# Query products of a two-layer graph transformer as pairs of tiles in seven quadrant products

## The chip, the core and the metric

The kernel runs on one core of a Trainium2 chip. The metric is device time in microseconds (us). The core has five engines that run their own streams of instructions and meet through semaphores: TensorE (PE; its weight loads are shown apart, as PEld), VectorE (DVE), ScalarE (ACT), GpSimd (POOL) and SyncE (SP), which here only issues DMA transfers. Operands lie in SBUF, 128 partitions wide; matmuls write into eight PSUM banks of 128 x 512 float32.

## The reference, cut to what matters

Two layers, each graph attention and a feed-forward block, on N = 2708 tokens of width 512, with 8 heads of 64 and a hidden width of 2048, all in float32. The adjacency matrix is sparse and differs per token.

```python
def layer(h, adj, Wq, bq, Wk, bk, Wv, bv, Wo, bo, W1, b1, W2, b2, ...):
    mask = adj.astype(float32) + eye(n)
    q = (h @ Wq.T + bq).reshape(n, 8, 64)
    k = (h @ Wk.T + bk).reshape(n, 8, 64)
    v = (h @ Wv.T + bv).reshape(n, 8, 64)
    scores = einsum('nhd,mhd->hnm', q, k) / sqrt(64)
    scores = where(mask[None] == 0, -1e9, scores)
    ctx = einsum('hnm,mhd->nhd', softmax(scores), v).reshape(n, 512)
    h1 = layer_norm(h + ctx @ Wo.T + bo, ln1_g, ln1_b)
    ff = relu(h1 @ W1.T + b1) @ W2.T + b2
    return layer_norm(h1 + ff, ln2_g, ln2_b)

x = layer(x, adj, *layer0);  x = layer(x, adj, *layer1)
```

The change touches only `q = h @ Wq.T + bq` with its factor of 1/8.

## The kernel before, in words

`by_edges` holds both layers. The tokens are 22 tiles of 128 (the last one has 20). For every token the kernel makes a list of its neighbours from the adjacency matrix, sorts the tokens by the length of their lists, and regroups them into 22 groups of like length. Attention then gathers the keys and values of a group's neighbours, two slots (`SLOTS`) at a time, from a table `kv_d` in DRAM; queries go through a table `q_d` in DRAM, and a group fetches the rows of its tokens. The order of all instructions is written out by hand: generators for attention (`attend`, moved on by `advance` and `until`), the feed-forward and the norms are interleaved with the products, and each engine runs its instructions in the order in which the Python code issues them. A tile pool with `bufs=n` has n buffers per tag; who asks for a buffer waits until everything that used it, transfers too, is through.

The work goes through these stages (times are those of the trace before):

- *Keys of layer 0* (0 to 154 us, `first`). A pair of tiles at a time, `xg` is loaded from the transposed input by SP (three buffers, tags w1_5 to w1_7; `load`, line 921). PE makes keys and values (`project`, line 616), ACT takes them out of PSUM, POOL adds the key bias (line 964), ACT's queue stores them to `kv_d`. Beside that `lists` (line 729) works on the adjacency rows: SP loads a half row block `aj` (line 737), POOL adds the diagonal (line 740), ACT turns it into codes (line 746), DVE finds the neighbours with MAX8 (line 751). At t = 19 to 21 `counted` and `ranked` (lines 766 and 827) sort the tokens: DVE's chain from line 772 to 813, and then a product on PE, `pr` (line 841), behind which PE's later work stands.
- *Queries of layer 0* (about 154 to 250 us, `first_queries`, line 996). `xg` is loaded a second time, each tile is one product of 4 x 128x512 by `wq`, DVE scales it by 1/8 and adds `bq` in one instruction (`evicted`, line 1001; `bq` is scaled once when it is loaded), two tiles share a buffer `qs` and are stored together. At t = 2 the last keys and the lists' placing are finished, and from then on attention of layer 0 is moved on between the tiles.
- *Feed-forward of layer 0* (250 to about 1050 us): 11 blocks of two groups, `blocks`, with the attention of the next block between its steps. Most of them already use a form with seven quadrant products (`feed_forward_by_seven`, line 1734). Each block's result gets its layer-1 keys and values one block later (`keys_values`, line 1858), which also stores its transposed tokens `zT` to `zT_d` in DRAM.
- *The border* (about 1050 to 1145 us): the last block's keys and values, then the queries of layer 1. Their tokens come back from `zT_d`; the first eight tiles are loaded ahead (`preloaded`, line 1428), others follow in streams of three (`queries`, line 1448). `query` (line 1462) is one tile: product, one eviction into a buffer `qs` with the tag `row` (three buffers, used by the residual rows of the feed-forward as well), and behind it `kept` (line 1475) issues the store of the tile before. Weights of the coming feed-forward are formed on DVE (`form_apart`, line 1688). Attention of layer 1 starts here (`next(ahead)`). Twenty of the 22 tiles are asked for here; the two of the block that ended last are asked for beside the first feed-forward block.
- *Feed-forward of layer 1* (1145 to 1815 us), like layer 0's.

An attention step (`Tile.weights` and `Tile.weigh`, lines 1154 and 1169) is a product of keys and queries on DVE (line 1156), a sum (1162), exponentials on ACT, products with values on ACT and DVE (1182, 1188) and an addition on DVE (1195).

These few lines carry the query path before:

```python
def evicted(t, q, qs):                                   # layer 0, line 1001
    nc.vector.scalar_tensor_tensor(
        qs[:r, t % 2], q[:r], DK**-0.5, bq[:r], ALU.mult, ALU.add)
...
qs = dn.tile([P, DM], F32, tag="row", name="qs", bufs=3) # layer 1, line 1462 on
nc.vector.scalar_tensor_tensor(qs[:r], q[:r], DK**-0.5, self.bq[:r], ALU.mult, ALU.add)
self.kept()
self.due = (g, qs)
```

Of the kernel before, what the change touches and what calls it, by code (L numbers as in the profile page):

```python
# [18 lines left out]
P = 128  # L19
# [27 lines left out]
OWN = 5  # L47
WARM = 7
# [439 lines left out]
def by_edges(ctx: ExitStack, tc: tile.TileContext, x, xT, adj, layers, out, redo):  # L488
# [150 lines left out]

    def finish(steps):  # L640
        for _ in steps:
            pass
# [274 lines left out]
    def first(w, meanwhile):  # L917
# [3 lines left out]
        def load(by=nc.sync):  # L921
# [5 lines left out]
            step = bw if i else P  # L927
            for a in range(0, bw, step):
                (by if a else nc.sync).dma_start(
                    out=t[:, :, a : a + step], in_=chunked(xT)[:, :, b + a : b + a + step]  # L930
                )
                yield
# [20 lines left out]
        done, before = 0, None  # L953
        for t in range(NT):
# [27 lines left out]
            meanwhile(t)  # L982
            if t == QT:
                wq = matrix(w, "Wq", "wq", nc.gpsimd)
            if t == NT - 4:
                bq = row_of(short[1], "bq", DK**-0.5)

# [6 lines left out]
        return bq, wq, parts, placing[1], pa, tokens, last_keys  # L994

    def first_queries(bq, wq, parts, inverted, pa, tokens, last_keys, meanwhile):

        nonlocal at
        made = []

        def evicted(t, q, qs):
            r = size(t)
            nc.vector.scalar_tensor_tensor(
                qs[:r, t % 2], q[:r], DK**-0.5, bq[:r], ALU.mult, ALU.add
            )
            plus_rest(qs[:r, t % 2], q, r, DK**-0.5)
# [11 lines left out]
        for t in range(NT):  # L1018
            r = size(t)
            q = project(tokens(t, 1), r, wq, "q", other=t % 2 > 0)  # L1020
# [18 lines left out]
            evicted(t, q, qs)  # L1039
# [33 lines left out]
    def own_query(g, zT, to, bq, wq):  # L1073
# [3 lines left out]
        nc.vector.scalar_tensor_tensor(to[:r], q[:r], DK**-0.5, bq[:r], ALU.mult, ALU.add)  # L1077
        plus_rest(to[:r], q, r, DK**-0.5)
# [279 lines left out]
    class Layer:  # L1358
        def __init__(self, n, w):
            self.n, self.w, self.w1, self.w2, self.due = n, w, [], [], None  # L1360
            self.stages = []
            self.apart, self.other = True, False
# [65 lines left out]
        def preloaded(self, tiles, temp):  # L1428

            places = []  # L1430
            for _ in range(2):
                both = at.tile([P, SLOTS, DM], F32, tag="acc", name="zTs", bufs=2)
                places += [both[:, i] for i in range(SLOTS)]
            places += [at.tile([P, DM], F32, tag="cx", name="zTs", bufs=CXB) for _ in range(CXB)]
            places.append(temp())
            places = [place.rearrange("p (c t) -> p c t", c=NC) for place in places]
            for g, place in zip(tiles, places):
                nc.sync.dma_start(out=place, in_=zT_d[self.n][g])
            return list(zip(tiles, places))

        def two(self, tiles):

            both = dn.tile([P, 2, NC, P], F32, tag="hT", name="zTs", bufs=1)
            for i, g in enumerate(tiles):
                nc.sync.dma_start(out=both[:, i], in_=zT_d[self.n][g])
            return both

        def queries(self, tiles):

            zTs = []  # L1450
            for i in range(len(tiles) + 1):
                while len(zTs) < min(i + 3, len(tiles)):
                    zT = dn.tile([P, NC, P], F32, tag="cT", name="zT", bufs=3)
                    nc.sync.dma_start(out=zT, in_=zT_d[self.n][tiles[len(zTs)]])
                    zTs.append(zT)
                yield
                if i < len(tiles):
                    self.query(tiles[i], zTs[i])
            self.kept()
            yield  # L1460

        def query(self, g, zT):
# [3 lines left out]
            q = project(lambda c: zT[:, c, :r], r, self.wq, "q", self.other and self.apart)  # L1466
            qs = dn.tile([P, DM], F32, tag="row", name="qs", bufs=3)
            nc.vector.scalar_tensor_tensor(
# [786 lines left out]
```

## Time and profile before

| | before |
|---|---|
| median of 3 runs | 1817.35 us (1817.26 to 1817.72) |
| the profiled execution | 1817.08 us, span of its instructions 1815.1 us |
| PE, matmuls | 1791.5 us busy, 99% of the span |
| PEld, weight loads | 1214.6 us, 67% |
| DVE | 1463.3 us, 81% |
| ACT | 1001.1 us, 55% |
| POOL | 855.4 us, 47% |
| DMA | 426.74 MB, mean 235 GB/s |
| mean granted clock of TensorE | 0.998 |

The span is the time from the first to the last instruction of the profiled execution; its own time is 2 us longer. Busy times are sums over the engine's instructions, those that only issue a transfer not counted. In the rows below, a timeline row has its start and its busy time in us, then the engine, the line of the kernel, the operation, its output and inputs by the program's names with their sizes, and the number of instructions put together; what stands in brackets at its end is the idle time ahead of it and what ended that. A row of a window has its length, then for PE, PEld, DVE, ACT and POOL the busy time and the count, the granted clock, the DMA share and GB/s. A row of transfers has the issuing queue and the number of issues, KB of each, and the median time from issue to landing.

### The profile page before, as it was taken

The numbers are of one execution on the slowest core, as the hardware profiler recorded it, in microseconds if no ns is written. First come the engines' busy times: TensorE is split into PE (matmuls) and PEld (weight loads), VectorE is DVE, ScalarE is ACT, GpSimd is POOL, SyncE is SP. The second block draws the span as 40 slices with busy tenths as digits, with TensorE's granted clock in tenths as the row PEclk, the third lists the DMA queues.
The fourth block names the chain that finished last, engine by engine and source line by source line (L and its number), as shares of the span: only waits on it lengthen the run. The fifth ranks groups of instructions, "written<-read, shape, count | busy, mean of one in ns | idle before, by whom it ended". The sixth has DMA issues, their size and how long they took to land. (4 is left out here: it accounts for less than half of the span.)

```text
span 1815.1 us, 23887 instructions
## 1 busy us (share of the span) xinstructions
PE 1791.5 (99%) x6839; PEld 1214.6 (67%) x6839; DVE 1463.3 (81%) x2599; ACT 1001.1 (55%) x3397; POOL 855.4 (47%) x830
## 2 busy tenths in 40 slices
PE   9999999999999999999999999999999999999997
PEld 4444456666777867777677644666666888788786
DVE  4987778988989889799896267988888899989933
ACT  5771436645555555555653104677776677767631
POOL 3333755534454544454540132556665665655312
PEclk9999999999999999999999999999999999999999
DMA  9997987757676675666752777967867787877531
GB/s 335 369 344 252 374 284 245 230 181 241 203 238 220 203 259 192 208 220 202 241 194 73 242 285 272 319 193 256 279 186 263 243 264 237 293 225 234 173 94 36
DMA packets 186728, 426.74 MB, mean 235 GB/s; under 512 B 20550, under 2 KB 83898, under 8 KB 186584
## 3 DMA queue, kind: packets, MB, share of 16 engines
q0 software_dynamic: 76992, 264.49, 44.0%
q1 hardware_dynamic: 99434, 139.01, 22.5%
q10 hardware_dynamic: 10158, 21.61, 3.1%
q8 instruction: 56, 0.92, 0.2%
q14 instruction: 88, 0.72, 0.1%
HBM read 357.13 MB, written 57.11 MB: 228 GB/s over the span
## 5 line engine op out<-in xcount | busy, mean ns | idle before, releaser
L1119 POOL DMA_INDIRECT kv<-kv_d,listed x420 | 526.0, 1252 | 307.2 <-DVE acc L1195 145.8
L1780 PE MATMUL pf<-hT,w 128*128 128x256 f32 x1792 | 407.2, 379 | 2.1 <-ACT ft L1791 2.1
L1780 PEld LDWEIGHTS pf<-hT,w 128*128 128x128 f32 x1792 | 339.2, 190 | 59.2 <-issue 11.0
L1182 ACT ACTIVATE kv<-kv,p 128x64 f32<-128x64 f32 x1232 | 311.0, 335 | 5.0
L1156 DVE TENSOR_TENSOR kv<-kv,q 128x1024 f32<-128x1024 f32 (+1 forms) x222 | 257.1, 1158 | 14.1 <-DMA q<-q_d,ident_i 10.9
L1162 DVE TENSOR_REDUCE sc<-kv 128x16 f32<-128x1024 f32 (+1 forms) x222 | 258.0, 1162 | 7.6
L1195 DVE TENSOR_TENSOR acc<-acc,kv 128x1024 f32<-128x1024 f32 (+2 forms) x178 | 205.6, 1155 | 49.6 <-ACT kv L1182 36.9
L1596 PEld LDWEIGHTS pf<-hT,w 128*128 128x128 f32 x1024 | 178.5, 190 | 55.3 <-issue 34.6
L1596 PE MATMUL pf<-hT,w 128*128 128x256 f32 (+1 forms) x1024 | 214.6, 357 | 0.1
L1791 ACT ACTIVATE ft<-pf,b 128x256 f32<-128x256 f32 x168 | 78.1, 466 | 214.1 <-PE pf L1780 211.4
L1569 PE MATMUL a<-w,ft 128*128 128x512 f32 x416 | 194.6, 592 | 0.0
L1175 ACT ACTIVATE p<-sc,listed 128x8 f32<-128x8 f32 x420 | 103.6, 295 | 127.9 <-DVE sc L1162 116.5
L1281 POOL TENSOR_TENSOR rd<-va,mhalf 128x1 f32<-128x1 f32 (+1 forms) x48 | 43.8, 913 | 230.8 <-DVE va L1279 230.7
L626 PE MATMUL o<-wo,cT 128*128 128x512 f32 x336 | 151.0, 593 | 0.3 <-ACT cT L1354 0.3
L1188 DVE TENSOR_TENSOR kv<-kv,p 128x512 f32<-128x512 f32 (+1 forms) x178 | 123.6, 694 | 4.8 <-ACT p L1175 4.5
L1569 PEld LDWEIGHTS a<-w,ft 128*128 128x128 f32 x416 | 77.7, 190 | 57.5 <-issue 52.0
L626 PEld LDWEIGHTS o<-wo,cT 128*128 128x128 f32 x336 | 63.4, 190 | 69.3 <-issue 59.6
L1331 POOL TENSOR_SCALAR va<-sq 128x1 f32<-128x1 f32 (+1 forms) x40 | 17.2, 429 | 188.4 <-ACT xb L1324 101.9
L751 DVE MAX8 tops<-code 128x8 f32<-128x247 f32 (+2 forms) x242 | 78.8, 400 | 28.0 <-ACT code L746 27.9
L1226 ACT ACTIVATE cx<-acc,su 128x64 f32<-128x64 f32 (+1 forms) x352 | 88.2, 333 | 11.2 <-DVE su L1218 6.2
L1182 ACT ACTIVATE acc<-kv,p 128x64 f32<-128x64 f32 (+1 forms) x352 | 88.8, 335 | 1.4
L746 ACT ACTIVATE code<-aj 128x1354 bf16<-128x1354 int32 (+1 forms) x44 | 73.5, 1724 | 23.7 <-POOL aj L740 19.0
(258 smaller groups left out, 2793.8 us busy)
## 6 DMA issues: line engine op xcount, KB each, us to landing
forms<-form_d SPq DMA_DIRECT2D x294, 128.0 KB, 3.8
aj<-in_adj SPq DMA_DIRECT2D x42, 677.0 KB, 6.3
kv_d<-kvs ACTq DMA_DIRECT2D x21, 512.0 KB, 7.4
h<-ln_b POOLq DMA_DIRECT2D x41, 256.0 KB, 7.0
xg<-in_xT SPq DMA_DIRECT2D x19, 512.0 KB, 8.0
w<-in_W SPq DMA_DIRECT2D x16, 512.0 KB, 6.4
kv<-kv_d,listed POOLq DMA_INDIRECT x420, 6.5
zT_d<-zT SPq DMA_DIRECT2D x22, 256.0 KB, 5.3
```

The source lines that it names most:

```text
L626: nc.tensor.matmul(o[:r], xs(c), wm[:, c, :], start=(c == 0), stop=(c == NC - 1))
L1119: return nc.gpsimd.indirect_dma_start(out=to, out_offset=None, in_=table[:, :], in_offset=bass.IndirectOffsetOnAxis(ap=s, axis=0), bounds_ ...
L1156: nc.vector.tensor_tensor(kv[:r, :c, :DM], kv[:r, :c, :DM], self.q[:r].unsqueeze(1).to_broadcast([r, c, DM]), ALU.mult,)
L1162: nc.vector.tensor_reduce(self.sc[:r, s0 : s0 + c, :], kv[:r, :c, :DM].rearrange("p s (h d) -> p s h d", d=DK), AX.X, ALU.add,)
L1175: nc.scalar.activation(p[:r, s, :], self.sc[:r, s, :], AF.Exp, bias=minus[:r, g, s : s + 1])
L1182: nc.scalar.activation(to[:, i, hd], kv[:r, i, DM + h * DK : DM + (h + 1) * DK], AF.Copy, scale=p[:r, s0 + i, h : h + 1],)
L1188: nc.vector.tensor_tensor(to[:, 0, :].rearrange("p (h d) -> p h d", d=DK), kv[:r, 0, DM:].rearrange("p (h d) -> p h d", d=DK), p[:r, s0, : ...
L1195: nc.vector.tensor_tensor(self.acc[:r, :c, :], self.acc[:r, :c, :], kv[:r, :c, DM:], ALU.add)
L1226: nc.scalar.activation(cx[:r, hd], self.acc[:r, 0, hd], AF.Copy, scale=self.su[:r, h : h + 1])
L1569: nc.tensor.matmul(a[:r, cols], fts[f][:, c0 : c0 + r], self.w2[f // 2][:, f % 2, cols], start=(f == 0), stop=(f == NFC - 1),)
L1596: nc.tensor.matmul(pf[:, :w], self.w1[f // 2][:, c, f % 2 * P : f % 2 * P + P], hT[:, c, :w], start=(c == 0), stop=(c == NC - 1),)
L1780: nc.tensor.matmul(pf[:, :W], self.w1[j][:, c, f % 2 * P : f % 2 * P + P], hT[:, c, :], start=(c == 0), stop=(c == NC - 1),)
```

## The change

Two tiles A and B of tokens (256 x 512) times the weights (512 x 512) are taken as a 2 x 2 by 2 x 2 product of quadrants, in the form of Strassen and Winograd: seven products of quadrants in place of eight, for four sums of token quadrants (`token_sums`), four sums of weight quadrants (`formed_of`) and additions behind the products. A quadrant product is two matmuls of 128x256, so that a pair has fourteen of these in place of eight of 128x512. `Seven` issues them in two parts: `first` (four products in the banks c0 and c1) with the additions `begun`, then `second` (three products in a0 and a1) with `ended`. Each pair takes four PSUM banks, two of pool f and g each or one of each and the two of `ps_a`, in turn.

- *Layer 0* takes the first ten tiles (five pairs) this way. Their token sums are formed on POOL in the keys' phase, behind the lists of each odd tile t, from the first load of `xg`, and kept in places that the feed-forward's weights take later. The products use one token quadrant (the first half of B's columns) only through the sums, so that the second load of these five pairs leaves it out and goes in two transfers. The weights are formed on POOL at t = 19, `wq` itself is scaled by 1/8 on ACT at t = 18, so that all evictions of queries lose their factor. One pair of loads of feed-forward weights moves from t = 10 to t = 11.
- *Layer 1* takes eighteen tiles, `order[2:20]` (nine pairs), by `half`, called twice per pair. Tokens are loaded ahead into other places (attention's buffers kv and cx, the tags hT, cT and h). The sums of the next pair are issued on POOL with the first half of a pair. The weights are formed on DVE (`form_queries`, and `form_first` in place), `wq` is scaled on ACT at f = 9 to 12 of the last block. The stores of a pair are issued at the first half of the next pair, ahead of its `begun`, which asks for two `row` buffers. The two tiles of the last block are asked for in `keys_values`, with the block's keys and values, and no longer beside the first feed-forward block.

```diff
+SUMS = ("w1_2", "w1_3", "w2_3", "w1_4", "w2_4")
+FORMQ = ("w2_2", "w1_1")
...
+    def formed_of(w, to, by):
+        b11, b12, b21, b22 = w[:, :2, :W2], w[:, :2, W2:], w[:, 2:, :W2], w[:, 2:, W2:]
+        t1, t2, t3, t4 = to
+        by.tensor_tensor(t3, b22, b12, ALU.subtract)
+        by.tensor_tensor(t1, b12, b11, ALU.subtract)
+        by.tensor_tensor(t2, b22, t1, ALU.subtract)
+        by.tensor_tensor(t4, b21, t2, ALU.subtract)
+    def token_sums(a, b, to, by):
...
+        by.tensor_tensor(s1, a21, a22, ALU.add)
+        by.tensor_tensor(s2, s1, a11, ALU.subtract)
+        by.tensor_tensor(s3, a11, a21, ALU.subtract)
+        by.tensor_tensor(s4, a12, s2, ALU.subtract)
+    class Seven:
...
+            self.first = (
+                (self.c0[:, L], a[:, :2, :], w[:, :2, L]),
+                (self.c0[:, R], s2, t2),
+                (self.c1[:, L], s1, t1),
+                (self.c1[:, R], s3, t3),
+            )
+            self.second = (
+                (self.a0[:, L], a[:, 2:, :], w[:, 2:, L]),
+                (self.a0[:, R], s4, w[:, 2:, R]),
+                (self.a1[:, L], b[:, 2:, :], t4),
+            )
...
+        def begun(self, q, bias, more, wide=None):
+            nc.vector.tensor_tensor(q[0], self.c0[:, L], bias[:, L], ALU.add)
+            nc.vector.tensor_tensor(q[3], self.c0[:, R], q[0], ALU.add)
+            nc.vector.tensor_tensor(self.c1[:, L], self.c1[:, L], more, ALU.add)
...
+            nc.vector.tensor_tensor(q[3], self.c1[:, L], q[2], ALU.add)
+        def ended(self, first, q2):
+            nc.vector.tensor_tensor(first, self.a0, first, ALU.add)
+            nc.vector.tensor_tensor(q2, self.a1[:, :W2], q2, ALU.add)
@@ first: load, and the keys' phase
+            if i >= XBS and i % XBS < len(SUMS):
+                src = chunked(xT)
+                nc.sync.dma_start(out=t[:, :2, :P], in_=src[:, :2, b : b + P])
+                nc.sync.dma_start(out=t[:, 2:, :], in_=src[:, 2:, b : b + bw])
...
+            if t % 2 and t // 2 < len(SUMS):
+                place = wts.tile([P, 4, 2, P], F32, tag=SUMS[t // 2], name="sums")
+                x2 = xg[t // 2]
+                sums.append([place[:, i] for i in range(4)])
+                token_sums(x2[:, :, :P], x2[:, :, P:], sums[-1], nc.gpsimd)
+            if t == QT + 2:
+                nc.scalar.activation(wq, wq, AF.Copy, scale=DK**-0.5)
...
+            if t == NT - 3:
...
+                formed_of(wq, forms, nc.gpsimd)
+                more = dn.tile([P, W2], F32, tag="hT", name="more", bufs=1)
+                nc.gpsimd.tensor_tensor(more, bq[:, W2:], bq[:, :W2], ALU.subtract)
@@ first_queries
+            elif t % 2 == 0:
+                x2 = xg[t // 2 + XBS]
...
+                q = Seven(x2[:, :, :P], x2[:, :, P:], sums[t // 2], wq, forms, banks)
+                q.products(q.first)
+            else:
+                q.products(q.second)
...
+                if t % 2 == 0:
+                    q.begun(quarters, bq, more, flat[:, W2 : 3 * W2])
+                else:
+                    q.ended(flat[:, :DM], quarters[2])
@@ class Layer
+        def form_queries(self):
...
+            nc.vector.tensor_tensor(t3, b22, b12, ALU.subtract)
+            nc.vector.tensor_tensor(t2, t3, b11, ALU.add)
+            nc.vector.tensor_tensor(t4, b21, t2, ALU.subtract)
+        def form_first(self):
+            w = self.wq
+            nc.vector.tensor_tensor(w[:, :2, W2:], w[:, :2, W2:], w[:, :2, :W2], ALU.subtract)
...
+        def summed(self):
...
+            token_sums(zA, zB, self.next_sums, nc.gpsimd)
+        def half(self, late=False):
+            def begun():
+                qs = [dn.tile([P, DM], F32, tag="row", name="qs", bufs=3) for _ in range(2)]
...
+            if self.one is None:
...
+                self.summed()
...
+                one.products(one.first)
+                self.kept()
+                self.one = one, tiles, None if late else begun()
+                return
+            one, tiles, qs = self.one
+            qs = qs or begun()
+            one.products(one.second)
+            one.ended(qs[0], qs[1][:, :W2])
+            self.due = list(zip(tiles, qs))
@@ keys_values
+                if asking:
+                    asking(g, zT)
+                else:
+                    nc.sync.dma_start(out=zT_d[n][g], in_=zT)
@@ the border, layer 1's side
             for j in (5, 6):
-                now.query(*pool.pop(0))
+                now.half()
                 now.form_apart(j)
             next(ahead)
...
+            for i in range(6):
+                if i > 1:
+                    advance(0.65)
+                now.half()
+            now.loaded(order[16:18], hTs())
+            for i in range(6):
+                now.half()
                 if i == 4:
                     now.stores = nc.sync
                 if len(got) < 2 or i < 3:
                     advance(0.65)
+            now.kept()
             until(blocks[0][0])
             early[n] = now.attended(blocks[0], got, None, True)
             next(early[n])
-            now.query(order[16], both[:, 0])
+            now.loaded(order[18 : 2 * AHEAD], last_places)
+            now.half(True)
...
-            now.query(order[17], both[:, 1])
+            now.half()
             advance(0.6)
-            next(streamed)
+            now.half()
             advance(0.6)
...
+            now.half()
+            now.kept()
@@ the border, layer 0's side
-            nxt.wq = now.wq
-            for _ in range(2):
-                nxt.query(*pool.pop(0))
-                if len(pool) % 2:
-                    next(behind)
+            nxt.loaded(order[10:12], hTs())
+            (one, other), zTs = nxt.units.pop(0)
+            nxt.query(one, zTs[0])
+            next(behind)
+            nxt.form_queries()
+            nxt.query(other, zTs[1])
             nxt.kept()
             for g in order[:2]:
                 own[g] = asked(n + 1, g)
             finish(behind)
+            nxt.summed()
+            nxt.kept()
...
             nxt.staged()
             for j in (3, 4):
                 nxt.form_apart(j)
+            nxt.form_first()
```

More of the change, by code (lines that the diff above doesn't have):

```diff
@@ L1361, in __init__ @@
             self.stages = []
+            self.units, self.one, self.forms = [], None, None
             self.apart, self.other = True, False
@@ L1426, in load_next, with loaded @@
             self.nbo = self.unsettled[-1][0]
-        def preloaded(self, tiles, temp):
-            places = []
-            for _ in range(2):
[L1432 to L1436, printed above, removed]
-            for g, place in zip(tiles, places):
[L1438 to L1460, printed above, removed]
+        def loaded(self, tiles, places):
+            zTs = []
+            for g, place in zip(tiles, places):
+                zT = place.rearrange("p (c t) -> p c t", c=NC)
+                nc.sync.dma_start(out=zT, in_=zT_d[self.n][g])
+                zTs.append(zT)
+            for i in range(0, len(zTs), 2):
+                self.units.append((tiles[i : i + 2], zTs[i : i + 2]))
         def query(self, g, zT):
@@ L2022, in beside_queries, with hTs @@
             early[0] = early[0], now.turned(blocks[0], early[0])
+    def hTs():
+        both = dn.tile([P, 2, DM], F32, tag="hT", name="zTs", bufs=1)
+        return [both[:, i] for i in range(2)]
     def temp():
@@ L2027, in by_edges @@
     first_queries(*first(layers[0], beside_keys), beside_queries)
-    behind, pool = None, []
+    behind = None
     for n in range(NL):
@@ L2032, in by_edges @@
         if n > 0:
-            streamed = now.queries(order[10:16])
             got = {}
```

171 lines of the change are left out of this document (121 added, 50 removed).

## The prediction

> **What bounds the kernel now.** I read the page, then the windows of the stretch where layer 0 hands over to layer 1 (the border), then each engine's timeline there and in the first 170 us. The page says TensorE:
>
> ```profile
> span 1815.1 us, 23887 instructions
> PE 1791.5 (99%) x6839; PEld 1214.6 (67%) x6839; DVE 1463.3 (81%) x2599; ACT 1001.1 (55%) x3397; POOL 855.4 (47%) x830
> PE 29%; DVE 5%; issue 3%; ACT 2%; DMA 2%; POOL 0%; SPq 0%; POOLq 0%; ACTq 0%; DVEq 0%
> 1070.00:1090.00 20.00, 20.00 (x48) 8.79 (x47) 9.54 (x19) 1.24 (x4) 10.13 (x10) 1.00 0.79 284
> 1090.00:1110.00 20.00, 20.00 (x48) 8.88 (x47) 18.75 (x26) 11.25 (x47) 8.31 (x8) 1.00 0.98 353
> 1110.00:1130.00 20.00, 17.84 (x48) 7.90 (x47) 9.80 (x15) 7.14 (x28) 0.00 (x0) 1.00 0.56 208
> 1130.00:1144.00 14.00, 14.00 (x41) 6.75 (x40) 11.84 (x19) 4.54 (x18) 5.60 (x6) 1.00 0.61 200
> 1144.00:1186.00 42.00, 41.70 (x154) 26.96 (x153) 39.98 (x50) 29.18 (x113) 24.85 (x20) 1.00 1.00 347
> ```
>
> PE is busy 99%, so a shorter PE should shorten the span. But the window rows (length; PE, PEld, DVE, ACT, POOL busy; clock; DMA share) show DVE at 18.75 of 20 us and 39.98 of 42 us just where layer 1's queries and first attention lie: DVE has some 14 us to spare there, all between 1110 and 1144, and none behind. Both places that the change touches are hand-overs in which PE runs level with another chain.
>
> **The change, part by part.**
>
> *Products.* A pair of query tiles was eight 128x512 matmuls and becomes fourteen 128x256 ones. Ten tiles of layer 0 are five pairs, eighteen of layer 1 nine.
>
> ```profile
> 1070.63 17.33 PE L626 MATMUL q<-wq,zTs 128*128 128x512 f32 x40
> 999.75 0.59 PE L1769 MATMUL a<-forms,ft 128*128 128x256 f32 x2
> 1002.34 0.59 PE L1769 MATMUL a<-w,forms 128*128 128x256 f32 x2
> 1003.19 0.69 DVE L1825 TENSOR_TENSOR u<-c,u 128x512 f32<-128x512 f32 x1
> 1003.80 0.41 DVE L1826 TENSOR_TENSOR h<-c,h 128x256 f32<-128x256 f32 x1
> 1004.13 0.68 DVE L1828 TENSOR_TENSOR h<-a,h 128x512 f32<-128x512 f32 x1
> 1101.58 1.88 DVE L1468 SCALAR_TENSOR_TENSOR qs<-q,bq 128x512 f32<-128x512 f32 x3
> ```
>
> Five tiles take 17.17 us without the drain, 3.43 each, 6.87 a pair. Six steps of 128x256 start from 999.75 to 1002.34: 0.432 each, 6.05 for fourteen. So a pair saves 0.82 us of PE: 4.1 us in layer 0, 7.4 in layer 1, 11.5 in all.
>
> *Evictions.* A tile cost one instruction of 0.6 us start to start (1101.58, three in 1.88), 1.2 a pair. The pair now needs `begun`'s five or six and `ended`'s two. From the rows, 128x512 is 0.6 (1003.19 to 1003.80), 128x256 0.33 (1003.80 to 1004.13); one that reads the instruction before it, about 0.5. That is near 3.4 us a pair: 2.2 more on DVE each.
>
> *Token sums of layer 0, on POOL in the keys' phase.* Four adds of 128x256: between 0.45 us (128x128) and 1.27 (128x512) below, so 0.7 each, 2.8 a pair, in slack of POOL. What isn't covered is the buffer. `x2` is the tile of xT that the next load but two overwrites; that load stands in SP's queue ahead of the adjacency loads, and now waits for POOL too.
>
> ```profile
> 33.87 3.60 PE L626 MATMUL k<-wk,xg 128*128 128x512 f32 x8
> 34.06 0.38 SPq L929 DMA_DIRECT2D xg<-in_xT  x1
> 37.05 8.01 SPq L737 DMA_DIRECT2D aj<-in_adj  x4
> 40.89 0.45 POOL L740 TENSOR_TENSOR aj<-aj,diag 128x128 int32<-128x128 int32 x1
> 45.21 1.27 POOL L964 TENSOR_TENSOR kvs<-kvs,bk 128x512 f32<-128x512 f32 x1 [3.86 <-ACT kvs L962]
> 46.58 0.45 POOL L740 TENSOR_TENSOR aj<-aj,diag 128x128 int32<-128x128 int32 x1
> 52.21 0.46 POOL L740 TENSOR_TENSOR aj<-aj,diag 128x128 int32<-128x128 int32 x1
> 81.61 3.56 DVE L751 MAX8 tops<-code 128x8 f32<-128x247 f32 x11
> 85.95 0.41 POOL L740 TENSOR_TENSOR aj<-aj,diag 128x128 int32<-128x128 int32 x1 [1.76 <-DMA aj<-in_adj]
> 86.64 3.56 DVE L751 MAX8 tops<-code 128x8 f32<-128x247 f32 x11
> 135.73 3.55 DVE L751 MAX8 tops<-code 20x8 f32<-20x247 f32 x11
> 140.80 0.84 DVE L772 TENSOR_SCALAR has<-top 128x528 f32<-128x528 f32 x1
> 150.05 0.71 DVE L813 TENSOR_TENSOR before<-before,run 128x528 f32<-128x528 f32 x1
> 151.04 0.61 PE L841 MATMUL pr<-before,ones 128*128 128x264 f32 x2
> aj<-in_adj SPq DMA_DIRECT2D x42, 677.0 KB, 6.3
> ```
>
> Before, SP's load of xT goes at 34.06, as PE leaves the pair (33.87), and the adjacency rows behind it are asked for at 37.05, 9.5 us before POOL uses them (46.58), which a landing of 6.3 us allows. After, the sums of that pair run only behind the list work at 40.89, to about 44.1; then xT, then the rows, which land 7 us after the sums. From one odd tile's list (40.89) to the next (52.21) are 11.3 us now; it becomes 2.8 + 7.0 + 5.6 (46.58 to 52.21) = 15.4. The first pair has slack and loses about 2.5, the other four about 4 each: the list at 85.95 comes 18 us late. Behind it DVE has nine lists of 5.03 us (81.61 and 86.64 to 135.73 go at that pitch where nothing waits); from 86.64 to 140.80 it needs 54.2 us and has to work 51, so about 3 us are made up. The counting at 140.80 is 15 us late. PE waits for its end: `before` is written by 150.76, and PE reads it at 151.04, a slack of 0.3 us. So +15.1. Bounds: 0 if the rows are early enough anyway, 19 with a landing of 7.2.
>
> *Weights formed on POOL at t = 19*: four adds of 1.25 us, one of 0.7, and the key bias, 6.9 us, beside DVE's small adds and copies of the counting. One row says what that does:
>
> ```profile
> 148.09 1.26 POOL L964 TENSOR_TENSOR kvs<-kvs,bk 128x512 f32<-128x512 f32 x1 [2.43 <-issue]
> 148.10 1.28 DVE L808 COPY run<-run 128x4 f32<-128x4 f32 x1
> ```
>
> A copy of four columns took 1.28 us, as long as POOL's add. Bounds 0 (no more such meetings) and 5.6 (each of POOL's instructions holds DVE once, 6.9 less the 1.3 there already); nearer neither, I take 2.5. The Trainium skill (SBUF — State Buffer, "Who interferes with whom") says that DVE instructions with two SBUF inputs, or in a two-port mode, and GpSimd instructions that read SBUF shut each other out for a whole instruction; the rows agree, and by the rule the term would be the full 5.6 and the total 1859.
>
> *PSUM of layer 0.* A pair takes four banks where two tiles took two. The third pair needs a bank of pool f while tile 21's values, pair 1's c0 and its a0 hold all three, so PE waits for the last addition:
>
> ```profile
> 165.46 10.57 PE L626 MATMUL q<-wq,xg 128*128 128x512 f32 x24
> 169.27 2.13 DVE L636 TENSOR_TENSOR kvs<-v,kvs 20x512 f32<-20x512 f32 x3
> ```
>
> PE would be there at 167.2 and DVE, about 0.9 us earlier than now, at 170.5: 3.3 us, of the 4.1 gained. The evictions' extra 2 us a pair fit DVE's waits for PE up to 191. The scale of wq on ACT, the smaller second loads of xT and the weight loads at t = 11 instead of 10 cost nothing: ACT and SP wait for PE there. Layer 0 in all: -4.1 + 15.1 + 2.5 + 3.2 = +16.7.
>
> *Layer 1's border.* `half` takes two of the three `row` buffers per pair. It asks for them right behind the line that issues the stores of the pair before: `begun`'s second instruction writes the second tile and waits for a store to land. Before, a tile's buffer came round three tiles later.
>
> ```profile
> 1086.80 1.23 DVE L1156 TENSOR_TENSOR kv<-kv,q 128x1024 f32<-128x1024 f32 x1 [1.54 <-DMA kv<-kv_d,listed]
> 1097.98 5.24 ACTq L1479 DMA_DIRECT2D q_d<-qs  x3
> 1108.00 0.69 DVE L1468 SCALAR_TENSOR_TENSOR qs<-q,bq 128x512 f32<-128x512 f32 x1 [0.49 <-DMA q_d<-qs]
> 1117.82 3.67 PE L626 MATMUL q<-wq,zT 128*128 128x512 f32 x8 [1.61 <-DVE acc L1195]
> 1143.89 0.69 DVE L1468 SCALAR_TENSOR_TENSOR qs<-q,bq 128x512 f32<-128x512 f32 x1 [0.63 <-PE q L626]
> DMA to landing us min/median/max: 2.6/4.8/6.0
> ```
>
> Even with three tiles' grace one eviction (1108.00) waited. Queued behind DVE's wait are the attention steps, and behind those ACT and PE. Count DVE from the first attention step (1086.80) to the last eviction before the feed-forward (1144.5): it was busy about 43 us, 9 of them fourteen evictions, so 34 of attention and norm. After, the step starts about 5.5 us later, at 1092.3: `form_queries` (three of 0.6), the queries of tiles 21 and 0 (3.4, moved here from beside the first block), `form_first`, which waits for PE and stands behind eight additions of `form_apart`, and two pairs with one store wait. Then 34, seven pairs of 3.4 = 23.8, and the store waits. A store lands 4.8 us after its issue; where an attention step lies between, 0.4 to 2 us are left (pairs 3, 4, 6 and 9: 4.8 together), where none does 4.2 and 4.6 (pairs 5 and 7), and the residual rows of the first block, which want two of the same buffers, add 5.9: 19.5. The end is 1092.3 + 34 + 23.8 + 19.5 = 1169.6. Before, it would be 1148.0 with the 3.4 us of the moved queries. So +22, in place of PE's -7.4, and the next 42 us, DVE full, give none back. Bounds: +2 with no store waits, +30 at a landing of 6.0 each. POOL's sums (2.8 a pair) stand in its queue between the gathers; they cost PE 1 to 2 us early, inside DVE's delay.
>
> *Sum*: 16.7 + 22 = +38.7 against the profiled execution's 1817.1 (span 1815.1 and 2.0 around it), 0.3 under the median of 1817.35: **1856 us**.
>
> **Rivals.** (1) *Faster*: the rows land early enough that neither SP nor DVE holds anything: 1817.1 - 11.5 = 1806. For it: PE's 99%, and DVE's idle third at 1110 to 1130. It decides if the adjacency landing stays under 4 us after the sums and stores under 3; against it stand 6.3 and 4.8. (2) *Layer 0 alone loses*: stores land behind attention steps, the border ends at +2: 1836. (3) *Layer 1 alone loses*: the lists are early enough, layer 0 gives -0.9: 1838. (4) *Nothing measurable*: small waits eat the gain, within 0.2%: 1817; 0.2%, 3.6 us, is about what a measurement of this kernel can tell.
>
> A further cost no row here has: the granted clock is 1.00 in all windows, and PE never idles longer than 1.61 us there (1117.82). The Trainium skill (TensorE: Matmul & The Clock Gate, Part 1) says that an idle window of about 3.4 us halves PE's clock until it has been busy for one; by that each long stall would cost an estimated 1.7 us more, about 7 for four, 1863. No run here shows it yet.
>
> **Chances.** Both lose: 0.45. Layer 0 alone 0.16, layer 1 alone 0.16, all slower: 0.77. Nothing measurable 0.06, faster 0.17. The range that leaves out the faster case and little at the top: 1815 to 1872; the likeliest case by its own bounds 1838 to 1872.
>
> **What would show it.** SP's loads of xT among the first five pairs would go some 10 us later than 34.06; the counting (now 140.80) near 156; PE idle before `pr` by over 10 us; DVE's `begun` released by the stores of `q_d`; the feed-forward of layer 1 starting over 30 us later than 1143.7, layer 0's part included. Query products at 0.43 us each would confirm the gain. The prediction is wrong if POOL does the sums as PE leaves each pair, or if stores land inside the attention steps.

## The result, and the profile after

The changed kernel takes **1869.83 us** (median of 4 runs, 1869.14 to 1871.43) against 1817.37 before: a ratio of 1.029, 95% interval 1.0272 to 1.0307. It is 52.5 us slower. Its page of the profile shows PE busy for more microseconds, and still for a smaller share of the span:

```profile
span 1867.4 us, 24395 instructions
PE 1798.3 (96%) x7007; PEld 1254.1 (67%) x7007; DVE 1503.5 (81%) x2682; ACT 1004.4 (54%) x3402; POOL 906.9 (49%) x892
```

To place the loss, take four marks in PE's timeline. These are their rows before (start, busy time, line, operation): the products behind the counting, the first feed-forward of layer 0, the last products of layer 0, the first feed-forward of layer 1. Two further rows are needed below, the ten small additions of the counting on DVE and layer 1's first gather on POOL.

```profile
144.15 2.39 DVE L789 TENSOR_TENSOR before<-before,hot 128x48 f32<-128x48 f32 x10
154.32 10.57 PE L626 MATMUL q<-wq,xg 128*128 128x512 f32 x24
249.93 7.17 PE L1596 MATMUL pf<-hT,w 128*128 128x256 f32 x32
1050.54 1.98 PE L1569 MATMUL a<-w,ft 128*128 128x512 f32 x4
1076.15 1.06 POOL L1119 DMA_INDIRECT kv<-kv_d,listed  x1 [3.42 <-issue]
1143.69 7.07 PE L1596 MATMUL pf<-hT,w 128*128 128x256 f32 x32
```

And the same places in the timeline of the changed kernel, layer 0 first:

```profile
31.03 0.38 SPq L1006 DMA_DIRECT2D xg<-in_xT  x1
43.21 0.45 POOL L811 TENSOR_TENSOR aj<-aj,diag 128x128 int32<-128x128 int32 x1
45.81 0.73 POOL L660 TENSOR_TENSOR sums<-xg,sums 128x256 f32<-128x256 f32 x1
46.57 0.38 SPq L1006 DMA_DIRECT2D xg<-in_xT  x1
47.05 2.19 SPq L808 DMA_DIRECT2D aj<-in_adj  x4
52.37 0.45 POOL L811 TENSOR_TENSOR aj<-aj,diag 128x128 int32<-128x128 int32 x1 [3.42 <-DMA aj<-in_adj]
153.88 0.87 DVE L843 TENSOR_SCALAR has<-top 128x528 f32<-128x528 f32 x1
157.26 9.38 DVE L860 TENSOR_TENSOR before<-before,hot 128x48 f32<-128x48 f32 x10
158.78 1.27 POOL L648 TENSOR_TENSOR forms<-wq 128x512 f32<-128x512 f32 x1
169.81 1.25 PE L912 MATMUL pr<-before,ones 128*128 128x264 f32 x2 [11.81 <-DVE before L884]
176.01 1.13 PE L685 MATMUL q<-wq,xg 128*128 128x256 f32 x4
192.41 1.74 PE L685 MATMUL q<-wq,xg 128*128 128x256 f32 x4 [3.21 <-issue]
272.65 7.17 PE L1753 MATMUL pf<-hT,w 128*128 128x256 f32 x32
```

SP's load of xT at 46.57 goes as POOL's sums end (45.81 + 0.73), the adjacency rows go behind it at 47.05, and POOL waits 3.42 us for them. The counting starts at 153.88 instead of 140.80. Its ten additions, beside POOL's `forms`, take 9.38 us instead of 2.39. PE waits 11.81 us for the end of the counting. Layer 0's feed-forward starts 22.7 us late.

The border:

```profile
1075.93 1.98 PE L1726 MATMUL a<-w,ft 128*128 128x512 f32 x4
1100.00 0.74 POOL L657 TENSOR_TENSOR sums<-zTs 128x256 f32<-128x256 f32 x1
1107.62 1.08 POOL L1235 DMA_INDIRECT kv<-kv_d,listed  x1 [0.15 <-issue]
1108.87 2.07 PE L685 MATMUL q<-wq,sums 128*128 128x256 f32 x4 [5.66 <-DVE wq L1588]
1122.66 1.21 DVE L1272 TENSOR_TENSOR kv<-kv,q 128x1024 f32<-128x1024 f32 x1
1133.24 2.07 PE L685 MATMUL q<-forms,sums 128*128 128x256 f32 x4 [4.16 <-POOL sums L658]
1147.57 0.42 DVE L693 TENSOR_TENSOR qs<-q,qs 128x256 f32<-128x256 f32 x1 [2.93 <-DMA q_d<-qs]
1148.33 1.03 PE L685 MATMUL q<-wq,zTs 128*128 128x256 f32 x4
1198.20 7.80 PE L1753 MATMUL pf<-hT,w 128*128 128x256 f32 x32
```

From the last products of layer 0 to the first feed-forward of layer 1 are 122.3 us (1075.93 to 1198.20) instead of 93.2. The waits of that stretch, summed by engine (waiting line, released by: us, times, longest):

```profile
PE q L685 <- POOL sums L658: 8.3, 3, 4.2
PE q L685 <- DVE wq L1588: 5.7, 1, 5.7
DVE qs L693 <- DMA q_d<-qs: 8.7, 4, 2.9
```

With the others (the largest is 5.1 us for a pair's additions on DVE) PE waits 25.3 us there, 2.9 before. The granted clock (the column behind POOL's) is no longer 1.00 in the windows either:

```profile
155.00:170.00 15.00, 3.06 (x9) 1.13 (x8) 14.35 (x30) 1.49 (x3) 10.68 (x12) 0.73 0.63 218
1100.00:1150.00 50.00, 39.14 (x152) 32.07 (x151) 38.84 (x71) 7.72 (x31) 36.06 (x40) 0.86 0.67 223
```

Four instructions of 128x256 (the rows count two for each matmul of the program) take 1.03 us (1148.33) and 2.07 us behind a wait (1108.87, 1133.24): half speed.

So the account by marks is: layer 0's start +22.7, lost between there and the last products +2.7, border +29.1, given back behind it -2.2 (where two queries no longer stand in the first block), together +52.3, the difference of the spans. Of the 2.7 us, 2.1 are lost by the first block's second output product (325.88 instead of 301.02); ahead of it PE waits 0.86 and 0.92 us for ACT, which it did not do before.

### The profile page after: what moved, and what is told of

It is laid out like the page before. It is cut to its first block, busy times and chain, and to the rows that moved or that the text cites. A ratio compares the mean times of both kernels' runs of the same rounds, so it can differ in the third digit from the quotient of the medians.

```text
span 1867.4 us, 24395 instructions
## 1 busy us (share of the span) xinstructions
PE 1798.3 (96%) x7007; PEld 1254.1 (67%) x7007; DVE 1503.5 (81%) x2682; ACT 1004.4 (54%) x3402; POOL 906.9 (49%) x892
## 4 chain that ended last, share of the span: by engine, by line
PE 66%; DVE 14%; issue 7%; DMA 5%; ACT 4%; POOL 3%; ACTq 0%; POOLq 0%; SPq 0%; DVEq 0%
PE pf L1937 16%; PE pf L1753 8%; PE a L1726 7%; PE c L1926 7%; PE o L628 6%; PE a L1926 5%; PE k L628 5%; PE v L628 4%; DVE kv L1272 2%; DVE sc L1278 2%; PE tp L1465 2%; PE q L685 2%; ACT kv L1298 1%; DMA q_d<-qs 1%; ACT code L817 1%
## 5 line engine op out<-in xcount | busy, mean ns | idle before, releaser
L1272 DVE TENSOR_TENSOR kv<-kv,q 128x1024 f32<-128x1024 f32 (+1 forms) x222 | 257.3, 1159 | 12.5 <-DMA q<-q_d,ident_i 12.2
L1342 ACT ACTIVATE cx<-acc,su 128x64 f32<-128x64 f32 (+1 forms) x352 | 88.2, 333 | 15.7 <-DVE su L1334 10.6
```

What stands on the lines that cost most here:

```text
L1272: nc.vector.tensor_tensor(kv[:r, :c, :DM], kv[:r, :c, :DM], self.q[:r].unsqueeze(1).to_broadcast([r, c, DM]), ALU.mult,)
```

## The experiments

Kernels were compared with the kernel before on the same chip. That one took 1817.4 to 1821.0 us by chip, so ratios are what to compare; the marks are from each run's one profile. The runs whose names start with l0_ have layer 0's part of the change alone, and all of them but l0_alone also have the move of sums_first; l1_alone has layer 1's part alone. Apart from that the edits against the changed kernel are short:

```diff
 sums_first: token sums ahead of the pair's lists
-            if t % 2 and t // 2 < len(SUMS):        # behind lists(t)
+            if t % 2 == 0 and t // 2 < len(SUMS):   # right behind xs = tokens(t, 0)
 forms early (l0_sums_forms, l0_fixed: QT = 14; l0_forms16, l0_banks, l0_own6: QT = 13)
-            if t == NT - 3:  forms = ...
+            if t == QT + 3:  forms = ...
 keys first (l0_fixed, l0_forms16)
-                inverted(parts); last_keys()
+                last_keys(); inverted(parts)
 banks (l0_banks, l0_own6)
-                if t % 4:
+                if t % 4 == 0:
 own6
-OWN = 5
+OWN = 6
 form_first (also in no_sums, no_sums_rooms)
             finish(behind)
+            nxt.form_first()
...
-            nxt.form_first()                        # behind form_apart(3), (4)
 no_sums: only the first pair's sums are formed
+            if i: return                            # in summed
 no_sums_rooms: every second pair's queries have a place of their own
+            room = wts.tile([P, 2, DM], F32, tag=f"w2_{NFC // 2 - 1}", name="qs")
 stores_soon: right behind ended, all on SP
+            self.kept()
-            now.stores = nc.scalar
```

**Each part alone.**

> The kernel before with the layer 0 part of the change alone; layer 1's queries are as before. Theory (the two places lose independently): the feed-forward of layer 0 starts 22.7 us later, as in the changed kernel (272.65 against 249.93), and nothing behind it makes that up: 1817.4 + 22.7 = 1840, up to 1843 with the 2.7 us that the changed kernel loses between 300 and 1050 us. Rival (the lateness is given back, because later stages have slack of their own): under 1825.

> The kernel before with the layer 1 part alone; layer 0's queries are as before. Theory: the stretch from the last block of layer 0 to the first feed-forward of layer 1 is 29.1 us longer (120.45 against 91.33), of which the first blocks give back 2 to 5, because two queries no longer stand in them: 1842 to 1846. Rival (the border is long only because layer 0 came late and left attention or loads behind): under 1830.

Layer 0 alone: 1846.52 against 1820.37, ratio 1.0149 (1.0133 to 1.0166), 26 us; its feed-forward starts at 274.82. Layer 1 alone: 1849.68, ratio 1.0161 (1.0145 to 1.0178), 29 us; its border is 1051.34 to 1174.33, 123.0 us. Both lose, each just under 1 us more than the upper end of what was expected, counted from the kernel before on their chip. 26 + 29 is near the 53 that 1.029 gives of 1820: the two places lose independently, and next to nothing gives the loss back.

**Layer 0, the load behind the sums.**

> The changed kernel with one move: the token sums of a pair of layer 0 are issued on POOL at the start of the pair's first tile, ahead of that tile's key bias and lists, and no longer behind the lists of its second tile; the same instructions otherwise. Theory (head of line on SP: the load of xT waits for POOL's sums, the adjacency rows wait behind it): the loads of xT go as PE leaves a pair, the counting starts at about 141 instead of 153.88, and the kernel gains about 13 us: 1857. Rival (the lists are late because POOL has 14 us more to do, or because the transfers themselves land later, 7.9 against 6.3 us): the counting stays within 4 us of 153.88 and the time above 1865.

Timeline of that run:

```profile
140.58 0.85 DVE L843 TENSOR_SCALAR has<-top 128x528 f32<-128x528 f32 x1
143.95 9.39 DVE L860 TENSOR_TENSOR before<-before,hot 128x48 f32<-128x48 f32 x10
156.51 1.25 PE L912 MATMUL pr<-before,ones 128*128 128x264 f32 x2 [5.51 <-DVE before L884]
201.33 0.22 PE L1514 MATMUL pr<-ident,temp 4*128 4x4 f32 x1 [3.91 <-DVE q L1193]
264.09 7.17 PE L1753 MATMUL pf<-hT,w 128*128 128x256 f32 x32
```

The same sums, one place earlier in the queue, and the counting starts at 140.58, where it was before the change (140.80): all 13 us of that lateness were the load that waited for POOL. POOL's additional work itself costs nothing there. The kernel gained less, 1864.56, ratio 1.0239 (1.0221 to 1.0256), some 9 us against 1.029, because a new wait of 3.91 us stands at the own queries (those of the first block, with which attention starts), with instructions at half speed behind it. The first feed-forward is 8.6 us earlier than in the changed kernel.

**Layer 0, the weights formed beside the counting.**

> The layer 0 part alone, with the token sums ahead of the lists (as in the run sums_first) and with wq loaded at t = 14 instead of 16, scaled at 16 and formed on POOL at t = 17, beside DVE's MAX8 and no longer beside the counting. Theory (the four forming additions on POOL and DVE's two-input additions hold each other up: ten small additions took 9.38 us beside them, 2.39 before): they take 2.4 to 3.6 us again, pr comes at about 151, and the first feed-forward about 6 us earlier than in sums_first (264.09), so 257 to 259; against the kernel before the loss falls from the 26 us of l0_alone to about 10. Rival (DVE's additions are slow for another reason, such as the late lists or the key bias on POOL): the ten additions stay above 8 us.

Ratio 1.0067 (1.0046 to 1.0089), 12 us over before instead of 26. But the additions are only half repaired:

```profile
141.62 0.19 POOL L798 COPY eighth<-tops 20x11 f32<-20x11 f32 x1 [4.03 <-DVE tops L822]
141.80 1.26 POOL L648 TENSOR_TENSOR forms<-wq 128x512 f32<-128x512 f32 x1
146.36 6.09 DVE L860 TENSOR_TENSOR before<-before,hot 128x48 f32<-128x48 f32 x10
158.11 1.25 PE L912 MATMUL pr<-before,ones 128*128 128x264 f32 x2 [7.63 <-DVE before L884]
```

The order of issue was earlier, the time was not: POOL's `forms` stand behind a copy that waits for DVE's last list, so they still begin with the counting. The next run but one moves them ahead of that copy.

> As l0_sums_forms, and in addition the last keys' additions stand ahead of the placing (inverted) instead of behind it, so that the PSUM bank which the third pair needs comes free earlier. Theory (PE's 3.21 us at the third pair is that bank, and half a clock for some 5 us follows): the wait goes, 4 to 5 us less than l0_sums_forms, the first feed-forward at 252 to 254, within 5 us of the kernel before or slightly ahead of it. Rival (the gathers start about 2 us later because the placing comes later, and the first attention step then stops DVE and PE): no gain over l0_sums_forms.

Ratio 1.0055 (1.0038 to 1.0072), first feed-forward at 255.54 against 260.23, later than the 252 to 254 expected: the late bank's wait fell to 0.42 us, and a wait of 1.73 us for gathered rows came up in its place, as the rival said in part. The two ratios overlap, so by the times the gain over l0_sums_forms is not shown.

> As l0_fixed, with wq loaded at t = 13, scaled at 15 and its forms issued on POOL at t = 16, ahead of the last copies that wait for DVE's lists, so that they end before the counting begins; in l0_fixed they still began at its start, and the ten small additions took 6.09 us, has 1.49. Theory (nothing but POOL's forming additions lengthens the counting): these take 2.4 and 0.85 us, PE waits less than 1.5 us for pr instead of 6.05, its half clock behind that goes, and the first feed-forward starts at 246 to 249, ahead of the kernel before (249.93): 1 to 4 us faster than before on the same chip, so a ratio of 0.998 to 1.0. Rival (PE's saved time is lost to attention's gathers, which start late): pr is early, but the first feed-forward stays above 252 and the ratio above 1.002.

```profile
143.73 3.32 DVE L860 TENSOR_TENSOR before<-before,hot 128x48 f32<-128x48 f32 x10
151.28 0.71 PE L912 MATMUL pr<-before,ones 128*128 128x264 f32 x2 [0.83 <-DVE before L884]
178.25 0.63 PE L1466 MATMUL tp<-ident,xr 128*128 128x128 f32 x4 [2.19 <-DMA xr<-in_x,ident_i]
196.18 1.78 PE L685 MATMUL q<-forms,xg 128*128 128x256 f32 x4 [3.16 <-DVE q L1194]
257.06 7.17 PE L1713 MATMUL pf<-hT,w 128*128 128x256 f32 x32
```

The first half of the theory held: without the forming beside it the counting takes 10.9 us from its start to `pr` (140.36 to 151.28), where it took 10.2 before the change and 15.9 in the changed kernel; the ten additions take 3.32. The second half fell: ratio 1.0061 (1.0048 to 1.0075), feed-forward at 257.06, as the rival said. PE now comes early to the own queries and waits for gathers, whose chain (counting, placing, rows, first attention step) is no shorter than before.

**Layer 0, can the saved PE time be used?**

> As l0_forms16, but the placing stands ahead of the last keys' additions again, and the third pair is kept off the late bank by the order of the banks instead: the first, third and fifth pair take two banks of pools f and g each, the second and fourth one of each and the two of ps_a. Theory (what l0_forms16 lost was the gathers: the placing came at 170.5 instead of 167, so the first rows for the own queries were 2.2 us late and the first attention step held DVE and PE 3.2 us and half a clock): the gathers start 3 us earlier, the first feed-forward at 250 to 253, ratio 0.999 to 1.003. Rival (the gathers' landing, not their start, sets it, or the bank wait comes back in another place): first feed-forward above 255, ratio above 1.005.

> As l0_banks, with the first block's own queries and the first attention step one tile later in the order (t = 6 and 7 instead of 5 and 6), so that PE, which gets there some 4 us earlier than before the change, has another tile's products ahead of them. Theory (PE's saved time is lost only because it waits for gathers that start no earlier than before): PE's waits at the own queries go, the first feed-forward at 246 to 249, ratio 0.997 to 1.000. Rival (attention starts as late as the gathers allow in any case, and moving it back makes it late for the first block): PE waits for the first block's attention instead, first feed-forward above 252, ratio above 1.002.

Timeline of l0_banks:

```profile
224.27 0.33 PE L1466 MATMUL tp<-ident,cx 128*128 128x128 f32 x1 [1.44 <-ACT cx L1343]
225.97 8.50 PE L628 MATMUL o<-wo,cT 128*128 128x512 f32 x16
253.56 7.17 PE L1713 MATMUL pf<-hT,w 128*128 128x256 f32 x32
1057.94 1.98 PE L1686 MATMUL a<-w,ft 128*128 128x512 f32 x4
```

and of l0_own6:

```profile
253.71 7.17 PE L1713 MATMUL pf<-hT,w 128*128 128x256 f32 x32
1075.51 1.98 PE L1686 MATMUL a<-w,ft 128*128 128x512 f32 x4
```

l0_banks has the ratio 1.0022 (1.0013 to 1.0032): with the queue, the forms and the banks repaired, layer 0's pairs still lose 4 us (the ratio lies in the theory's range, the first feed-forward, at 253.56, just above it), and the 4.1 us that PE saves do not arrive. By 218.80 PE stands where it stood before the change (218.79): `pr` came 0.9 us later (151.93), and waits of 0.97 and 0.30 us for DVE and 0.68 us for ACT are new. Then PE meets the first block's attention (`cx`, 1.44 us, and a slow group behind it), which it did not wait for before. l0_own6 reaches the feed-forward at the same time, as its rival said, and ends the layer 17.6 us later (1075.51 against 1057.94): ratio 1.0139 (1.0121 to 1.0156). Between the two marks its PE waits 7.9 us for attention (`cx`), for which l0_banks does not wait there at all; the rest of the 17.6 us was not told apart. That fits a start of attention, behind counting, placing and gathers, that runs level with PE in the query stretch; no run here starts it earlier, so it is not shown what that would give. Of the 3.8 us that l0_banks takes more than the kernel before from the first feed-forward to the last products (804.4 against 800.6), 1.9 are lost in the first block (its second output product starts at 306.51, 301.02 before), much as in the changed kernel; the rest stays open. The two profiles are of different chips, and the kernel before is itself 3.6 us slower on that one (1821.01 against 1817.37).

**Layer 1, one delay at a time.**

> The changed kernel with one move at the border: the in-place subtraction in wq (form_first) stands right behind the last block's queries, ahead of the eight subtractions of form_apart, instead of behind them. Theory (PE idles 5.66 us for it, and is at half its clock for some 6 us behind it): PE's wait goes, and the first feed-forward of layer 1 starts 6 to 8 us earlier relative to the end of layer 0: 1862 to 1864. Rival (DVE's chain with the stores and evictions sets the end of the border, so that PE's early wait is hidden): within 2 us of 1869.8.

PE's 5.66 us for `wq` are gone, and the time is the same, ratio 1.0296 (1.0278 to 1.0313). Waits of that run's border:

```profile
PE q L685 <- POOL sums L658: 15.3, 4, 5.6
DVE qs L693 <- DMA q_d<-qs: 13.4, 5, 4.2
```

They were 8.3 and 8.7. The rival held: PE's wait moved to the next hold-ups, and DVE's waits for stores grew as well.

> The changed kernel with layer 1's stores of a pair issued right behind its last addition, all on SP's queue, instead of behind the next pair's first products, partly on ACT's. Theory (DVE waits 8.7 us for the stores of the pair before, and work queues behind): these waits fall below 4 us and the border (122.3 us) gets 4 to 8 us shorter. Rival (PE's waits for POOL's sums and the gathers decide): DVE's store waits fall, but the border stays within 2 us.

Ratio 1.0296 (1.0274 to 1.0319). DVE's store waits fell from 8.7 to 6.0 us, and the border is 120.7 us (1074.56 to 1195.30), 1.5 less. The rival held. With 6.0 us of store waits left, the run does not show what their end alone would give.

> The run form_first, with the token sums of layer 1's pairs left out but for the first pair's, which all nine pairs use; everything else is as there. Theory A (POOL's queue, sums ahead of the gathers and gathers ahead of the sums, carries the border): PE's 15.3 us of waits for sums go, the gathers start about 3 us earlier, and the border (123.6 us in form_first) falls by 10 to 16 us. Theory B (DVE's chain of evictions and store waits sets the end, and POOL's delays lie inside it): less than 5 us.

Ratio 1.0277 (1.0254 to 1.0299); border 119.2 us (1075.60 to 1194.75) against 123.6 in form_first, 4.4 less, which is theory B. What took the place:

```profile
DVE qs L693 <- DMA q_d<-qs: 15.9, 5, 4.9
```

With POOL's sums out of the way DVE waits 15.9 us for the stores of the pair before, 13.4 in form_first. By the times the gain is within the noise, for the ratios overlap (1.0296 and 1.0277). One more run took the store waits away too.

> As no_sums (form_first, and all nine pairs of layer 1 use the first pair's token sums, the others are left out), and in addition every second pair's queries go into a place of their own of two tiles, which the left-out sums would have used, so that no pair waits for the stores of the pair just before it. Theory (with POOL's sums gone the store waits of 15.9 us are the border's largest part, and they and POOL's queue hid each other, which is why taking away either alone gave 1.5 and 4.4 us): DVE's store waits fall below 3 us and the border from 119.2 to 104 to 108 us; what is left over the 91.3 us of the kernel before is DVE's 16 us of additional evictions less its spare time there. Rival (attention's gathers and the half clock carry the border): above 114 us.

Ratio 1.0219 (1.0202 to 1.0236):

```profile
1078.06 1.98 PE L1732 MATMUL a<-w,ft 128*128 128x512 f32 x4
1184.14 9.14 PE L1759 MATMUL pf<-hT,w 128*128 128x256 f32 x32
```

No store wait is left, and the border is 106.1 us, as the theory said. Stores sent earlier gave 1.5 us and left-out sums 4.4; the sums left out and the store waits gone gave 17.5 of form_first's 123.6, and here the ratio falls clear of noise as well. What the store waits would give with the sums in place no run shows. Still 12.9 us over the 93.2 of before remain (the 91.3 of the expectation counts the same stretch of before from 1052.36, the last preloaded queries), and the run's PE timeline says of what: 4.4 for the queries moved in (3.4 and 1.0 of PE), less the 7.4 that the pairs save, 9.6 more of waits (12.5 against 2.9), and some 6.3 for instructions at half speed (106.1 - 12.5 = 93.6 us without the waits; at full speed it would be before's 93.2 - 2.9, and + 4.4 - 7.4, so 87.3). Of the 12.5 us of waits 10.6 are for DVE's additions of the pairs (lines 693 and 705). So even with free sums and free stores the pairs lose at this place, and what PE waits for there is mostly DVE's evictions.

No version here beats the kernel before.

## Why the prediction was right, and where it was short

It forecast slower by both places, 1856 us in 1815 to 1872; 1869.83 lies at the upper end, 13.6 us above by the spans (52.3 against 38.7). By its steps:

- *Products*: 6.05 us a pair, as measured in undisturbed pairs (1117.70 to 1123.74 in the changed kernel); the saving of 0.82 is real, and none of it arrived.
- *Evictions*: 3.4 us of DVE a pair, as measured (eight additions from 1139.19 to 1142.58).
- *The load behind POOL's sums*: forecast a pitch of 15.4 us, measured 15.9 on average over the five loads that wait (31.03 to 94.59); the counting 15.1 us late, measured 13.1. The last of these loads is 19.3 us late (75.26 before), so that some 6 us were made up and not 3. sums_first shows the mechanism.
- *Forms beside the counting*: the mis-sized term. Taken as 2.5 us in bounds of 0 to 5.6; the counting's start to `pr` took 15.9 us instead of 10.2, so 5.7, and l0_forms16, whose forms end before the counting, has 10.9. The choice between the bounds was a guess from one row with one meeting of POOL and DVE, though ten small two-input additions stand in the chain. The Trainium skill (SBUF — State Buffer, "Who interferes with whom") says that DVE instructions with two SBUF inputs contend with GpSimd instructions that read SBUF, under an exclusive lock; read as one lock-out for each of POOL's instructions, that gave 5.6 in the prediction. Here the trace agrees: 9.38 us against 2.39 for the ten additions.
- *The granted clock*: not in the sum, and it was there. From `pr` to the first query 6.2 us instead of 3.3, behind the late bank another 1.7 (192.41 to 197.6 for products that take 3.5). At the border PE's work at full speed would be 91.3 - 2.9 of waits - 7.4 saved + 4.4 moved in = 85.4 us, counted from the last queries of the preload (1052.36 to 1143.69); the changed kernel needs 95.1 without its waits (1077.75 to 1198.20, less 25.3), so some 9.7 us went to the half clock. Together with layer 0's 4.6 that is 14.3 us. The Trainium skill (TensorE: Matmul & The Clock Gate, Part 1) says that the clock falls to half after an idle window of about 3.4 us; here waits of 5.66 and 4.16 us were followed by half speed, and one of 3.07 us (ahead of 1158.47) as well. The prediction's estimate from it, 7 us, was low: half speed stood behind seven stalls and not four, at some 2 us each and not 1.7.
- *PSUM*: 3.3 us forecast (3.2 in its sum), 3.21 measured.
- *Layer 0 in all*: 16.7 forecast, 22.7 measured. The 6.0 between them are the forms' 3.2, the clock's 4.6 and the load's -2.0, to 0.2. Another 2.7 us were lost behind it, which no step had.
- *Border*: 25.1 us more forecast (DVE's last eviction ends at 1169.6 instead of 1144.5), 29.1 measured between PE's marks: near, but in part by luck, for two terms were wrong in opposite directions and the half clock was not in it. The first attention step was to be 5.5 us late and came 10.5 late (1122.66, less 25.4, against 1086.80). DVE does not idle ahead of it, so it was not the gathers that it waited for, but what stands before it on DVE. The eight subtractions of `form_apart` take 6.0 us beside POOL's sums of two pairs (1102.13 to 1108.13; the sums run from 1100.00 to 1107.5), where they took 3.2 before (1068.01 to 1071.2), and behind them DVE waits 3.15 us for the late products (1112.75). So POOL's sums did cost DVE time here; the prediction had called their cost 1 to 2 us inside DVE's delay. The store waits were 8.7 us and not 19.5; with PE's wait for `wq` gone they were 13.4, with the sums left out too 15.9. no_sums_rooms shows that the sums and the store waits together carry 17.5 us.
- *Given back*: 3.5 forecast by the moved queries (1148.0 against 1144.5), 2.2 measured. Border and giving back come to 21.6 (1169.6 - 1148.0), which its sum takes as 22.

The rivals: *faster* failed at its stated condition, rows under 4 us behind the sums: they came 5.8 us behind (46.54 to 52.37). Each place alone loses, so neither of the one-sided rivals was it, and 52.5 us is far from *nothing measurable*.

## What to carry to other kernels

An engine that reads 99% busy need not be what the span hangs on: look, at the places a change touches, for the chain that runs level with it, for only the slower of the two is worth shortening. An addition to a queue's work is cheap or dear by where it stands: ask what the next load waits for, and what is queued behind that load. And when removing one wait gives nothing, look where it went before calling it harmless: the 5.66 us of PE's wait for `wq` came back as longer waits for sums and stores, and only the run without both made the border clearly shorter.

## What the runs showed of the hardware

A PE wait of 1.44 us in l0_banks was followed by slow matmuls: the group at 225.97 above took 8.50 us, where the same group took 7.13 in the kernel before. Yet a wait of 2.54 us in the changed kernel was followed by one group at full speed (1.03) and only then by a slow one (1.86). A wait of 1.80 us (ahead of 1169.58) was not followed by half speed at all (1.13 and 1.03). So the length of a single wait does not tell whether the clock falls.
